# A one-core attention and mixture-of-experts kernel: the fourth chunk's sines and rotation after the third chunk's copies, and the output rows scaled one loop step later

## The chip, the cores and the metric

The kernel runs on one core of one Trainium2 chip. The metric is the device time of one launch in microseconds (us), the median over runs. A profile is one further execution, seen by the hardware profiler; its span runs from the first instruction to the last. Engines are called as in the profile: PE (matmuls), PEld (weight loads of PE), DVE (vector), ACT (scalar), POOL, and SP, which issues most DMAs. Each works through its own queue in order.

## What is computed

The input is x of 16 sequences with 512 rows of 128 numbers, all in float32. One layer is computed:

```
q, k = silu(x Wq), silu(x Wk), 16 heads of 8, rotated: [t*cos(ang), t*sin(ang)]
v    = x Wv
out  = (tril(q k^T) v) Wo * sigmoid(x G1 G2)      # linear attention, causal
x1   = layernorm(x + layernorm(out)*gamma + beta)
shared = (silu(x1 sg) * (x1 su)) sd               # for every row
routed = sum over the 2 best of 8 experts, 1280 rows per expert at most
y    = layernorm(x1 + shared + routed)
```

## The kernel before, in words

The 8192 rows are 64 chunks of 128 rows, four chunks to a sequence (`NC` = 4, `B` = 16, `NT` = 64). The order of the instructions on PE, ACT, DVE and POOL is the order in which the program writes them (`manual_schedule`), so every change of place in the code is a change of place in a queue.

**The attention loop** (L847 to L887) runs t from 1 to 64. In pass t it projects chunk t+2 (`project`: matmuls `products`; on ACT `squash`, `gate` and `spread`; on DVE `turn`, which writes the rotated `hat`), transposes chunk t+1 and copies it out of PSUM on ACT (`turn_over`: kT, q, qT), forms the causal products of chunk t (`energies`: 32 matmuls `pe` L526, four masked copies `et` L534 on DVE), and from them the output of chunk t-1 (`values`) and the running state (`remember`). Four of the eight PSUM buffers (`ps_w`) are handed round among all these tiles, so the projection of the next chunk waits until the copy `qT` (L488) has emptied an earlier buffer. The cosines and sines of the four chunk positions are made once, by `sines(c)` (one Abs and four Sin on ACT, L323 to L331), and `same(c)` on DVE duplicates them. For c = 3 this happens in pass t = 1, inside `project(3)`, and so ahead of the copies of chunk 2 on ACT; `turn(3)` follows it on DVE, ahead of the masked copies of chunk 1.

**The shared expert** is a list `feed` of small steps, 24 for each sequence: eight gate steps (`gate_half`: two matmul records L137 on PE and a Silu `sl` L139 on ACT), eight up steps (`up_half`: L150 on PE and the product `h` L151 on DVE), and eight down steps (`down_half`: L160; every second one ends with the addition L165 on DVE, which frees one of two PSUM buffers). They are written as 4 up-phase steps, then the 8 down steps of the sequence before, then 12 more up-phase steps.

**The expert phase** begins with six such steps, interleaved with expert 0's preparation in three parts of 512, 512 and 256 rows: `clear_rows` (L949, DVE) puts zero into unused rows, `turn_rows` transposes on PE (L960) and copies on DVE (L961). Then come eight experts, in which PE has no pauses.

**The tail** (L1106 to L1130) is the subject of two of the edits. Here 102 steps of `feed` are left. Each turn of the loop writes one of them, counts it in `begun`, and then writes some finishing work, if it has become due:

- `add_up(b)`: two additions L1017 on DVE that add the two routed rows of each token of sequence b; the second one also issues the load of a later sequence's rows.
- `finish_lot`: the last layernorm of four chunks. Four pairs of statistics (L105 and L107, DVE), the variance plus epsilon (`ve` L111, DVE), the power of minus one half on POOL (`rstd` L113), at least three steps later the product `nb` (L1041, DVE), then four scaled rows `res` (L1044, ACT) and a DMA of them (L1049, SP).

`an_end` advances the first of three running lots that isn't waiting; it is called up to twice in a turn, as often as `due` allows. `due` grows in each turn by the lots that are left times 9, divided by the steps that are left less 2. In the notation of the prediction a step is g, u or d with its sequence and number (u13.0 is the first up step of sequence 13; d12.2.0 is the first half of the third chunk's down product of sequence 12).

## Time and profile before

| | us |
|---|---|
| median of 3 runs | 841.85 (841.46 to 845.71) |
| the profiled execution, whole | 843.22 |
| its span | 841.5 |
| what lies outside the span | 1.7 |
| PE busy, of the span | 812.7 |
| DVE busy | 519.6 |
| ACT busy | 440.7 |
| POOL busy | 370.5 |
| attention, with the first shared steps | 0 to about 517 |
| experts | about 520 to 738 |
| tail | about 738 to 841.5 |

The profile gives each instruction a line of the kernel, the tiles that it writes and reads, and the idle time of its engine before it, with what ended that. A table of stretches gives the busy time of each engine and the clock that was granted to PE (1.00 is full). A list of waits gives who waited for whom: microseconds in total, times, longest. The timeline gives the start, the duration, the engine, the line, the operation and its tiles; an entry such as `[2.32 <-ACT qT L488]` at the end of a row says that the engine had been idle for 2.32 us and which instruction ended that.

### The profile page before, as it was taken

To read this page: it belongs to the slowest core of one execution; us is meant where nothing else is said; L and a number is where in the kernel's file an instruction comes from. 1 tells how busy PE (TensorE), PEld (TensorE's weight loads), DVE (VectorE), ACT (ScalarE), POOL (GpSimd) and SP (SyncE) were. 2 spreads that over 40 slices of the span, in tenths; PEclk is the share of its full clock that TensorE was granted. 3 is DMA by queue.
4 is the path that set the end of the run, shared out by engine and by line. 5 is a ranking of instruction groups with operands and counts; after the bars stand their busy time and mean duration, and the time that the engine had idled before them with its cause. 6 is when DMAs were issued, how large, how long until landed. Compare 5 with 4: busy or idle time off the path is not lost.

```text
span 841.5 us, 25752 instructions
## 1 busy us (share of the span) xinstructions
PE 812.7 (97%) x10290; PEld 555.6 (66%) x10290; DVE 519.6 (62%) x1603; ACT 440.7 (52%) x1413; POOL 370.5 (44%) x516
## 2 busy tenths in 40 slices
PE   6989999999999999999999999999999999999887
PEld 4766677668668667666666664766776677766555
DVE  7787777889977779965433335444344444247885
ACT  8677777786777778644222222333333333324545
POOL 2243333332377777878766570333333334312210
PEclk9999999999999999999999999999999999999999
DMA  6011111111111110075000015122321210034642
GB/s 205 23 35 35 35 34 34 35 34 34 32 44 60 50 52 30 26 269 204 25 11 7 2 29 144 32 83 92 98 76 43 92 63 30 26 109 138 177 124 63
DMA packets 66378, 57.54 MB, mean 68 GB/s; under 512 B 6164, under 2 KB 55116, under 8 KB 66258
## 3 DMA queue, kind: packets, MB, share of 16 engines
q1 hardware_dynamic: 59456, 44.95, 17.4%
q0 software_dynamic: 6656, 10.69, 3.7%
q8 instruction: 81, 1.33, 0.6%
q14 instruction: 39, 0.32, 0.1%
q10 hardware_dynamic: 146, 0.26, 0.1%
HBM read 32.62 MB, written 26.48 MB: 70 GB/s over the span
## 4 chain that ended last, share of the span: by engine, by line
PE 78%; DVE 13%; ACT 6%; issue 2%; POOL 0%; DVEq 0%; ACTq 0%; POOLq 0%
PE pd L160 11%; PE pu L150 10%; PE pg L137 10%; PE ped L984 8%; PE peg L1079 8%; PE peu L1081 8%; PE pq L426 5%; PE pe L526 3%; PE pt L479 3%; PE pout L559 2%; DVE h L151 2%; DVE et L534 2%; DVE st L105 2%; PE pst L500 2%; PE po L574 2%
## 5 line engine op out<-in xcount | busy, mean ns | idle before, releaser
L746 POOL DMA_INDIRECT xg_dram<-x,idx x128 | 130.2, 1017 | 41.0 <-issue 37.0
L990 POOL DMA_INDIRECT y_dram<-y,to x80 | 77.4, 967 | 160.9 <-ACT y L988 160.9
L151 DVE TENSOR_TENSOR h<-sl,pu 128x512 f32<-128x512 f32 x128 | 87.7, 686 | 89.3 <-PE pu L150 56.3
L139 ACT ACTIVATE sl<-pg 128x512 f32<-128x512 f32 x128 | 75.3, 595 | 122.0 <-PE pg L137 109.7
L160 PE MATMUL pd<-sd_sb,h 128*128 128x128 f32 x1024 | 125.4, 278 | 7.7 <-DVE x1T L165 7.5
L137 PE MATMUL pg<-x1T,sg_sb 128*128 128x512 f32 x256 | 131.7, 596 | 0.9 <-DVE h L151 0.8
L150 PE MATMUL pu<-x1T,su_sb 128*128 128x512 f32 x256 | 131.0, 593 | 0.0
L160 PEld LDWEIGHTS pd<-sd_sb,h 128*128 128x128 f32 x1024 | 120.8, 194 | 14.5 <-DVE x1T L165 8.4
L1084 DVE TENSOR_TENSOR eh<-esl,peu 128x512 f32<-128x512 f32 (+1 forms) x96 | 57.5, 599 | 109.7 <-PE peu L1081 98.7
L113 POOL TENSOR_TENSOR rstd<-ve,neghalf 128x4 f32<-128x4 f32 x47 | 49.2, 1046 | 142.8 <-DVE ve L111 107.0
L984 PEld LDWEIGHTS ped<-rd,eh 128*128 128x128 f32 x640 | 84.0, 192 | 24.1 <-issue 22.0
L534 DVE TENSOR_TENSOR et<-pe,causal 128x256 f32<-128x256 f32 x256 | 90.4, 416 | 4.8 <-PE pe L526 4.7
L511 POOL TENSOR_TENSOR state<-state,add 128x128 f32<-128x128 f32 x96 | 51.6, 538 | 76.5 <-DVE add L509 68.9
L1079 PE MATMUL peg<-xgT,rg 128*128 128x512 f32 (+1 forms) x192 | 84.6, 522 | 0.0
L1081 PE MATMUL peu<-xgT,ru 128*128 128x512 f32 (+1 forms) x192 | 84.4, 521 | 0.0
L984 PE MATMUL ped<-rd,eh 128*128 128x128 f32 x640 | 84.3, 275 | 0.0
L1083 ACT ACTIVATE esl<-peg 128x512 f32<-128x512 f32 (+1 forms) x96 | 50.6, 527 | 55.6 <-PE peg L1079 52.9
L150 PEld LDWEIGHTS pu<-x1T,su_sb 128*128 128x128 f32 x256 | 45.7, 190 | 44.4 <-issue 39.1
L988 ACT ACTIVATE y<-ped,wt 128x128 f32<-128x128 f32 x80 | 29.5, 369 | 85.6 <-PE ped L984 85.6
L137 PEld LDWEIGHTS pg<-x1T,sg_sb 128*128 128x128 f32 x256 | 44.1, 191 | 36.5 <-issue 32.3
L426 PE MATMUL pq<-W,xT 128*128 128x384 f32 x128 | 61.2, 561 | 5.8 <-ACT qT L488 4.6
L466 DVE TENSOR_TENSOR hat<-qk,cst_tok 128x512 f32<-128x512 f32 x64 | 46.4, 726 | 25.5 <-ACT qk L438 25.1
(184 smaller groups left out, 1266.3 us busy)
## 6 DMA issues: line engine op xcount, KB each, us to landing
y_dram<-vpad SPq DMA_DIRECT2D x16, 512.0 KB
y<-y_dram SPq DMA_DIRECT2D x32, 256.0 KB
xT<-xt SPq DMA_DIRECT2D x15, 384.0 KB
xg<-xg_dram SPq DMA_DIRECT2D x8, 660.0 KB
x<-x SPq DMA_DIRECT2D x16, 256.0 KB
o<-res SPq DMA_DIRECT2D x15, 256.0 KB
xg_dram<-x,idx POOLq DMA_INDIRECT x128
rg<-rg SPq DMA_DIRECT2D x8, 256.0 KB
```

The source lines that it names most:

```text
L137: nc.tensor.matmul(pg, sg_sb[:, ts(i, P)], seq, start=True, stop=True)
L139: nc.scalar.activation(sl, pg, AF.Silu)
L150: nc.tensor.matmul(pu, su_sb[:, ts(i, P)], seq, start=True, stop=True)
L151: nc.vector.tensor_tensor(h[i // half][:, i % half, :], h.pop(("s", i)), pu, ALU.mult)
L160: nc.tensor.matmul(pd, h[k][:, i - k * half, ts(c, P)], sd_sb[:, i, :], start=(i == 0), stop=(i == IS // P - 1))
L426: nc.tensor.matmul(pq[:, :, 0:24], xts[b][:, c, 0:P], W[:, 0:384].rearrange("p (h n) -> p h n", n=24), start=True, stop=True)
L534: nc.vector.tensor_tensor(et.rearrange("p s i n -> p (s i) n"), pes[a, half].rearrange("p s i n -> p (s i) n"), causal.unsqueeze(1).to_bro ...
L746: i = nc.gpsimd.indirect_dma_start(out=xg_dram[:, :], out_offset=bass.IndirectOffsetOnAxis(ap=idx[:, k, t : t + 1], axis=0), in_=x1[:, t, ...
L984: nc.tensor.matmul(pd, h[:, i, ts(c, P)], got[e][2][:, i, :], start=(i == 0), stop=(i == IR // P - 1))
L990: i = nc.gpsimd.indirect_dma_start(out=y_dram[:, :], out_offset=bass.IndirectOffsetOnAxis(ap=to[:, at : at + 1], axis=0), in_=y, in_offset ...
L1079: nc.tensor.matmul(pg[:, :n], rg_sb[:, ts(i, P)], xgTs[e][:, ds(o0, n)], start=True, stop=True)
L1081: nc.tensor.matmul(pu[:, :n], ru_sb[:, ts(i, P)], xgTs[e][:, ds(o0, n)], start=True, stop=True)
```

## The change

There are four edits. (1) `project(t)` no longer makes the sines and the rotation of chunks 0 to 3; those of chunk 3 are written in pass t = 1 after `energies(1)`, and so after the copies of chunk 2. In pass t = 2 `energies(2)` stands at the head of the pass, ahead of `project(4)`. (2) In `finish_lot`, after `nb`, at least one further step of `feed` is written before the scaled rows. (3) At the beginning of the expert phase the clearing of expert 0's third part stands behind the transposes and the copy of its first part. (4) The divisor of `due` is the number of steps that are left less 8, where it was less 2.

```
@@ project @@
-            if t == NC - 1:
-                sines(t)
-            turn(t)
+            if t >= NC:
+                turn(t)
@@ attention loop @@
                 stopped("wait")
+                if t == 2:
+                    energies(t)
                 if coming:
...
                 advance(turns)
-                if here:
+                if here and t != 2:
                     energies(t)
+                if t == 1:
+
+                    sines(NC - 1)
+                    turn(NC - 1)
                 if stopped("exp"):
@@ finish_lot @@
             nc.vector.scalar_tensor_tensor(nb, mv[:, :, 0], -1.0, rs, ALU.mult, ALU.mult)
+
+            at = begun
+            while not roots and feed and begun < at + 1:
+                yield False
             res = fp.tile([P, n, D], F32, tag="res", name=f"res_{lot[0]}")
@@ expert phase @@
-            for n_before, cleared in ((4, parts[:2]), (2, parts[2:])):
-                for _ in range(n_before):
-                    feed.pop(0)[2]()
-                for o0, n in cleared:
-                    clear_rows(0, o0, n)
-            for o0, n in parts:
-                turn_rows(0, o0, n)
+            for _ in range(4):
+                feed.pop(0)[2]()
+            clear_rows(0, *parts[0])
+            clear_rows(0, *parts[1])
+            for _ in range(2):
+                feed.pop(0)[2]()
+            turn_rows(0, *parts[0])
+            clear_rows(0, *parts[2])
+            turn_rows(0, *parts[1])
+            turn_rows(0, *parts[2])
             targets_of(0)
@@ tail @@
-                due += len(ends) * steps_each / max(len(feed) - 2, 1)
+                due += len(ends) * steps_each / max(len(feed) - 8, 1)
```

## The prediction

> **What bounds the kernel.** I read the page first (busy times, the slices, the chain that ended last).

> ```profile
> PE 812.7 (97%) x10290; PEld 555.6 (66%) x10290; DVE 519.6 (62%) x1603; ACT 440.7 (52%) x1413; POOL 370.5 (44%) x516
> ...
> PE   6989999999999999999999999999999999999887
> ...
> PE 78%; DVE 13%; ACT 6%; issue 2%; POOL 0%; DVEq 0%; ACTq 0%; POOLq 0%
> ```

> PE has work in 97% of the span, and only the first slices and the last three fall below nine tenths. So an edit can gain what PE stands idle there, and little else. I then went through PE's idle times in the timeline: 2.32 us at 19.4 to 21.7, and in the tail 1.93, 2.80 and 2.56 us, all before a down product L160. The list of waits for 740 to 842 says who causes these.

> ```profile
> ACT res L1044 <- DVE nb L1041: 34.6, 16, 5.0
> ...
> DVE h L151 <- ACT sl L139: 9.1, 8, 1.6
> ...
> PE pd L160 <- DVE x1T L165: 7.5, 4, 2.8
> ```

> PE waits 7.5 us for DVE's L165, and DVE itself, though late, stands idle 9.1 us in eight waits for an `sl` of ACT. The timeline of 754 to 772 shows such a wait and what becomes of it.

> ```profile
> 758.01 0.16 DVE L1041 SCALAR_TENSOR_TENSOR nb<-mv,rstd 128x4 f32<-128x4 f32 x1
> ...
> 758.20 0.88 ACT L1044 ACTIVATE res<-x1T,nb,rstd 128x128 f32<-128x128 f32 x2 [2.29 <-DVE nb L1041]
> ...
> 758.99 0.58 ACT L139 ACTIVATE sl<-pg 128x512 f32<-128x512 f32 x1
> ...
> 759.60 0.69 DVE L151 TENSOR_TENSOR h<-sl,pu 128x512 f32<-128x512 f32 x1 [1.43 <-ACT sl L139]
> ...
> 764.75 0.26 DVE L165 TENSOR_TENSOR x1T<-pd,x 128x128 f32<-128x128 f32 x1
> ...
> 765.07 5.47 PE L160 MATMUL pd<-sd_sb,h 128*128 128x128 f32 x32 [1.93 <-DVE x1T L165]
> ```

> ACT has `res` at its head, idle until `nb`; the `sl` behind it, whose matmul ended at 757.0, starts at 758.99; DVE idles 1.43 us; the lateness reaches L165 and PE. The other two stalls:

> ```profile
> 790.64 2.05 PE L160 MATMUL pd<-sd_sb,h 128*128 128x128 f32 x16 [2.80 <-DVE x1T L165]
> ```

> ```profile
> 814.77 4.11 PE L160 MATMUL pd<-sd_sb,h 128*128 128x128 f32 x32 [2.56 <-DVE x1T L165]
> ```

> The clock also counts. In the table of stretches it is halved after the stall at 763 and not after that at 788:

> ```profile
> 765.00:767.00 2.00, 1.93 (x11) 1.94 (x11) 1.72 (x7) 1.21 (x4) 1.01 (x1) 0.62 0.61 183
> 767.00:769.00 2.00, 2.00 (x11) 2.00 (x11) 0.48 (x2) 2.00 (x6) 0.00 (x0) 0.52 0.60 166
> ...
> 791.00:793.00 2.00, 1.84 (x17) 1.65 (x16) 1.86 (x10) 0.00 (x0) 0.23 (x1) 1.00 0.69 187
> ```

> **Edit 1, the start.** These are its rows:

> ```profile
> 18.87 0.36 ACT L323 ACTIVATE scratch<-scratch 128x192 f32<-128x192 f32 x1
> ...
> 20.28 0.37 ACT L481 COPY kT<-pt 128x256 f32<-128x256 f32 x1
> ...
> 21.08 1.41 DVE L534 TENSOR_TENSOR et<-pe,causal 128x256 f32<-128x256 f32 x4
> 21.27 0.38 ACT L488 COPY qT<-pt 128x256 f32<-128x256 f32 x1
> ...
> 21.71 1.65 PE L426 MATMUL pq<-W,xT 128*128 128x384 f32 x2 [2.32 <-ACT qT L488]
> ```

> The five sines hold ACT from 18.87 to 20.25, ahead of copies whose transposes had ended at 17.6. With the copies first, kT starts at 18.88, q at 19.14 and qT ends at 20.24 (21.65 now). DVE's `et` of chunk 1 start at 19.0, not 21.08, and end at 20.4. `energies(2)`, now at PE's head, needs q (20.0) and those `et`, and ends near 21.0; `project(4)`, behind it, starts there instead of 21.71. It takes 2.1 us now, at half clock after the idle time, and 1.14 at 26.43 at full clock. PE's idle time shrinks to 0.6, so I take 1.14: ACT's Silu of chunk 4 starts at 22.1, not 23.82. But sines and rotation come later: sines 20.25 to 21.63, `hat` of chunk 3 to 22.45 (now 21.16), its transposes near 23.1, and behind ACT's `spread` its kT at 23.5, where it is 25.05 now. The gain is **1.5 us**; at half clock it would be 0.6, and it can't exceed 2.9 (the idle time less 0.3, and 0.9 of slow projection). From there to 738 PE and the loop PE-ACT-qT set the pace, POOL's scatters hang on them, and the loads were issued long before, so the shift stays. SP's loads keep their order, since `energies` issues none.

> **Edit 3.** PE's third transposes now wait for the copy of part 1 (ends 519.88, they start at 519.93). Then they wait for the clearing of part 3, behind that copy: 518.84 + 0.60 + 0.43 = 519.87. **0.0**.

> **Edit 4** moves nothing. With 18 lots and 88 steps left `due` grows by 18*9/86 = 1.9 a turn and more later, and a turn uses two at most; counted through, only the 13th turn has one call where it now has two, and at that time every lot waits for its additions. The order written is the same. So the ends don't come sooner.

> **Edit 2** is what matters. I counted the loop through, before and after (for before this gives the order in which DVE's rows stand). `nb` keeps its place or moves a step, up to two statistics that followed `res` now stand directly behind it, and the `sl` of a gate step comes ahead of `res`. No instruction is added. DVE's starts lie apart by 0.60 (h, addition), 0.41 (statistics pair), 0.08 (nb), 0.1 (ve), 0.2 (L165); an `h` can start 1.13 after its up product does, an `sl` 1.06 after its gate product, and `res` takes 0.40 each.

> *First stall.* nb 758.01 stays. sl of g13.0 goes at 757.0, ahead of `res`. DVE does two statistics (to 758.9), h (759.5), addition (760.1), ve. ACT does `res` four times from 758.2 and the next sl to 760.35, so the last h starts at 760.4 instead of 761.82; the same 2.93 of work to L165 gives 763.3 for 764.75. The stall is 0.5, **1.4 less**. The next four half steps took 5.30 (765.07 to 770.37); four at full clock (0.89) take 3.57. After idle times of 0.85 and 0.89 (511, 519) the rows show 1.00, so I take the clock to stay full: **1.7**, bounds 0 and 1.7. DVE waits for PE there in either order, so the lateness starts anew at 0.

> *Second.* From the last L165 of sequence 12 to the first of 13 DVE has 17 statistics pairs, 8 additions and 8 h, before and after. Now it takes 19.55, of which 2.01 is waiting for `sl`. After, laid out in the same way, 0.55 is lost before the first h (two statistics that filled that time moved behind it) and 0.1 later. L165 comes 1.35 sooner; with half of the small waits among the following half steps (4.10 for 3.57) I count **1.9**.

> *Third.* DVE's wait is 2.61 of 18.86 now. After, one pair more, one wait of 0.55 (an `sl` behind two `res`), and a start 0.4 less late: L165 at 812.2 on the present scale, a stall of 0.2 to 0.3. With the small waits that follow (0.37, and 0.17 before 830.91) **2.8**.

> The tail's sum is 1.4 + 1.7 + 1.9 + 2.8 = 7.8; the most is 9.7 (7.5 of stalls, 1.7 of clock, 0.5), the least, if only the first stall shrinks, 1.4. What hides `res` coming later: at the end the last full lot's four rows end at 833.0 and ACT's next need is at 834.09. Each output DMA goes one or two steps later on SP, and a load may queue behind it, but a pair loaded at 752.4 is used at 764.9, 12 us later. If that cover were gone, DVE would wait at an addition.

> Sum: 1.5 + 0.0 + 0.0 + 7.8 = **9.3**. The profiled execution took 843.22 (span 841.5 and 1.7), which gives 833.9; the median is 1.4 lower and gives 832.6. I take **833.0**.

> **Rivals.** *(a) The clock falls elsewhere.* A stall of about 1.4 remains at 788, and the halved rows follow 1.93 but not 2.80, so length doesn't decide. If the halved stretch moves there and the start stays slow, the gain is 9.3 - 1.7 - 0.9 = 6.7: 835.4. [...]

> *(b) DVE is too late for the new place.* If `nb` runs over one half step (0.86) late, ACT stands at `res` as before, and the sl behind it waits. If stalls two and three stay, 1.5 + 1.4 + 1.7 = 4.6, without the clock 2.9: 837 to 839. For it: DVE is up to 4.6 late (pu ended at 808.5, h at 813.15). Against it: in my layout only one such wait is left.

> *(c) Slower.* The same lateness, but with four `res` in a row ahead of an `sl`, as at 827.33, where DVE idled 1.61. It decides when 8 of 14 lots pay it (12.9 against 9.1 now); with 12, 19.3 - 9.1 - 1.5 = 8.7 more: 850.5. My layout has four in a row for the lots at 758 and 808, ended in time.

> That edit 4 doesn't do what it says is in the forecast.

> **Chances.** Forecast 0.54 (its own range 829.5 to 836), (a) 0.17, (b) 0.21, (c) 0.08. Half a per cent is 4.2 us, about what a measurement of this kernel can tell from no change. Faster by more: forecast, (a) and a little of (b), 0.75; within: the rest of (b), 0.17; slower: 0.08. The low end 829.5 has the largest gains, 2.9 + 9.7 = 12.6 off 841.85, rounded up; the high end 838.5 takes in most of (b).

> **What would show it.** In the profile after: PE's idle time before L426 near 20 falls from 2.3 to 0.6 and the clock there stays at 1.00; DVE's wait for `sl` falls from 9.1 to below 3 and PE's wait for L165 from 7.5 to about 2; 765 to 770 has no halved clock; 517 to 738 is unchanged. I am wrong if DVE still waits for `sl` behind `res`, if additions wait for loads, or if the shift at the start is gone by 60 us.

## The result, and the profile after

| | before | after |
|---|---|---|
| median, us | 843.69 (841.46 to 845.71, 4 runs) | 833.06 (832.61 to 833.59, 4 runs) |
| ratio of the times | | 0.9876, 95% interval [0.9853, 0.9900] |
| the profiled execution, whole | 843.22 | 833.16 |
| its span | 841.5 | 831.4 |

The changed kernel is faster by 1.2%. To see where the time came from, I took matmuls that both kernels have and compared their starts in the two profiles. The projection of chunk 5 starts 2.20 us sooner, the work at 403 us 1.68 sooner, and the first expert's products behind edit 3 (at 520 us in the profile of before) 1.61 sooner. Nothing is gained or lost up to the tail (1.62). The tail gives the rest. The table cuts it at the third gate step of each sequence (g13.2 starts at 770.37 in before and at 765.66 in after), so each of the first three stretches holds one of the three stalls:

| us | g12.2 to g13.2 | g13.2 to g14.2 | g14.2 to g15.2 | g15.2 to the end | sum |
|---|---|---|---|---|---|
| before | 24.70 | 24.37 | 23.97 | 22.80 | 95.84 |
| after | 21.61 | 22.33 | 21.08 | 22.36 | 87.38 |
| gained | 3.09 | 2.04 | 2.89 | 0.44 | 8.46 |

1.62 and 8.46 make the 10.1 by which the spans differ. From the page of after, PE's row and the chain of work that ended last:

```profile
PE 810.5 (97%) x10290; PEld 554.8 (67%) x10290; DVE 519.3 (62%) x1603; ACT 439.6 (53%) x1413; POOL 369.0 (44%) x516
...
PE 82%; DVE 10%; ACT 5%; issue 1%; DMA 0%; DVEq 0%; ACTq 0%
```

PE has the same number of instructions and 2.2 us less of busy time (two halved-clock stretches are gone and one is new, below), and its share of the chain has grown from 78% to 82%: the kernel is nearer to what PE needs. The list of waits of after for the tail (us in total, times, longest):

```profile
ACT res L1053 <- DVE nb L1046: 17.9, 11, 4.2
...
DVE h L151 <- ACT sl L139: 1.9, 3, 1.0
...
PE pd L160 <- DVE x1T L165: 1.6, 2, 1.2
```

The first row was 34.6, the second 9.1 in eight waits, the third 7.5 in four. ACT still waits 17.9 us for `nb`, and that costs nothing any more, because DVE hardly waits behind it. The timeline of after shows the place where the first stall was:

```profile
756.39 0.15 DVE L1046 SCALAR_TENSOR_TENSOR nb<-mv,rstd 128x4 f32<-128x4 f32 x1
...
756.58 1.65 ACT L1053 ACTIVATE res<-x1T,nb,rstd 128x128 f32<-128x128 f32 x4 [0.57 <-DVE nb L1046]
...
758.13 0.57 ACT L139 ACTIVATE sl<-pg 128x512 f32<-128x512 f32 x1
...
758.74 0.69 DVE L151 TENSOR_TENSOR h<-sl,pu 128x512 f32<-128x512 f32 x1
...
761.67 0.26 DVE L165 TENSOR_TENSOR x1T<-pd,x 128x128 f32<-128x128 f32 x1
...
761.99 0.71 PE L160 MATMUL pd<-sd_sb,h 128*128 128x128 f32 x4 [0.46 <-DVE x1T L165]
```

`nb` is where it was (758.01 less the 1.62). ACT waits 0.57 for it, not 2.29, since the `sl` that stood behind `res` was done before. DVE's `h` has no idle time ahead of it, and PE's stall is 0.46 where it was 1.93. The stretches of after (us; busy time of PE, PEld, DVE, ACT, POOL; granted clock; DMA share; GB/s):

```profile
46.00:48.00 2.00, 2.00 (x44) 1.34 (x46) 1.97 (x6) 1.96 (x11) 0.00 (x0) 0.50 0.03 4
...
763.00:765.00 2.00, 2.00 (x21) 2.00 (x20) 1.40 (x5) 1.35 (x4) 0.69 (x1) 1.00 0.14 38
765.00:767.00 2.00, 2.00 (x12) 1.28 (x11) 1.52 (x7) 1.86 (x5) 0.00 (x0) 1.00 1.11 333
```

Behind the shorter stall the clock is full (it was 0.62 and 0.52). At 46 us it is halved once, where before had none. The projection at 47.00 us of before comes 2.26 sooner in after, the work at 61 us 1.33 sooner, so this stretch cost 0.9 us. At the start, the timeline of after:

```profile
18.80 0.37 ACT L480 COPY kT<-pt 128x256 f32<-128x256 f32 x1
...
19.97 1.06 PE L525 MATMUL pe<-q,kT 32*64 32x128 f32 x32 [0.68 <-ACT q L485]
...
20.95 0.91 PE L425 MATMUL pq<-W,xT 128*128 128x384 f32 x2
...
23.34 0.37 ACT L480 COPY kT<-pt 128x256 f32<-128x256 f32 x1
...
24.23 0.91 PE L425 MATMUL pq<-W,xT 128*128 128x384 f32 x2
```

The copy of chunk 2 starts at 18.80 and no longer at 20.28; the energies stand ahead of the projection, with 0.68 idle for 2.32, and the projection runs at full clock (0.91 for 1.65).

### The profile page after: what moved, and what is told of

The parts are those of the page before. It is cut to its first block, busy times and chain, and to the rows that moved or that the text cites. A ratio compares the mean times of both kernels' runs of the same rounds, so it can differ in the third digit from the quotient of the medians.

```text
span 831.4 us, 25754 instructions
## 1 busy us (share of the span) xinstructions
PE 810.5 (97%) x10290; PEld 554.8 (67%) x10290; DVE 519.3 (62%) x1603; ACT 439.6 (53%) x1413; POOL 369.0 (44%) x516
## 3 DMA queue, kind: packets, MB, share of 16 engines
q8 instruction: 81, 1.33, 0.7%
## 4 chain that ended last, share of the span: by engine, by line
PE 82%; DVE 10%; ACT 5%; issue 1%; DMA 0%; DVEq 0%; ACTq 0%
PE pd L160 13%; PE pu L150 11%; PE pg L137 11%; PE ped L989 9%; PE peg L1091 8%; PE peu L1093 8%; PE pq L425 5%; PE pe L525 3%; PE pt L478 3%; PE pout L558 3%; DVE et L533 2%; PE pst L499 2%; DVE h L151 2%; PE po L573 2%; DVE st L105 1%
## 5 line engine op out<-in xcount | busy, mean ns | idle before, releaser
L139 ACT ACTIVATE sl<-pg 128x512 f32<-128x512 f32 x128 | 76.0, 594 | 129.1 <-PE pg L137 114.4
L151 DVE TENSOR_TENSOR h<-sl,pu 128x512 f32<-128x512 f32 x128 | 87.5, 684 | 83.6 <-PE pu L150 57.4
L160 PE MATMUL pd<-sd_sb,h 128*128 128x128 f32 x1024 | 122.9, 276 | 1.7 <-DVE x1T L165 1.6
L160 PEld LDWEIGHTS pd<-sd_sb,h 128*128 128x128 f32 x1024 | 118.9, 192 | 7.8 <-issue 5.3
```

The lines of the kernel that those rows point to most:

```text
L139: nc.scalar.activation(sl, pg, AF.Silu)
L151: nc.vector.tensor_tensor(h[i // half][:, i % half, :], h.pop(("s", i)), pu, ALU.mult)
L160: nc.tensor.matmul(pd, h[k][:, i - k * half, ts(c, P)], sd_sb[:, i, :], start=(i == 0), stop=(i == IS // P - 1))
```

## The experiments

The theory under test: **the tail's gain comes from one place in one queue**. `res` stood at ACT's head before its `nb` was done, the Silu behind it came late, DVE waited for it and PE for DVE. The rivals: the gain comes from DVE's new order (the statistics that now stand behind `nb`); any delay of the lot's end gives it, however it is made; or the clock gives most of it. Smaller questions are whether edits 1, 3 and 4 do what the prediction says, and what still holds the tail back.

The kernels ran in three sets of four, each set on a chip of its own with the kernel before beside it, whose medians were 840.74 (23 runs), 843.50 (17 runs) and 840.68 (11 runs). Each ratio is against the kernel before of its own set.

### Edit 1 alone (set 1)

The diff is that of edit 1 in the change; the rest is before.

> Edit 1 alone on the kernel before. My theory (each edit pays for itself): the start gains 2.2 us at 26 us, as in the profile after, and 1.3 to 2.2 us of it reach the tail, depending on whether the clock is halved once more near 47 us; the tail keeps its three stalls of 1.9, 2.8 and 2.6 us and its 9.1 us of waiting for sl; in all 1.3 to 2.2 us less than before. Rival (the halved clock at 765 to 769 belongs to the phase of the kernel's clock window and not to the length of the stall): with the shift of the start alone the halved stretch at 765 vanishes, and the gain is 3.0 to 3.9 us.

Measured: 839.32, ratio 0.9979 [0.9967, 0.9991], 1.4 us below before. In its profile the work at 61 us is 2.43 sooner, and the tail shows the old stalls: 1.92, 2.79 and 2.30, with 8.9 us of waits `h <- sl`. But one thing was added there. From the stretches of this kernel:

```profile
787.00:789.00 2.00, 2.00 (x9) 2.00 (x10) 1.86 (x9) 0.00 (x0) 0.00 (x0) 0.50 0.78 217
```

The clock is still halved behind the stall of 1.92, so the rival, by which that halved stretch goes when the start shifts, did not come. (The clock window that the expectation names is seen in the profile of before as a grid: the halved stretches start at 11.15, 21.39 and 765.50 us, whole periods of 3.41 us apart.) It is now also halved behind the stall of 2.79, which went free in before (2.80 there), and that stretch of the tail took 25.37 for 24.37. The tail's code and the stall are the same; only the time at which they come has moved. Edit 1 alone thus gives what was forecast, and it can be taken back in part by where the clock falls.

### Edit 2 alone (set 1)

The diff is that of edit 2; the rest is before.

> Edit 2 alone on the kernel before. My theory: 7.8 to 8.5 us less; the stalls in the tail become 0.5, 1.2 and 0, DVE waits under 2.5 us for sl, and the clock at 765 to 769 is full because the stall before it is short. Rival (the phase of the clock window): the stall of 0.5 is followed by a halved clock as before, and the gain is 6.1 to 6.8 us.

Measured: 832.93, ratio 0.9904 [0.9887, 0.9920], 7.8 us below before. Its four stretches of the tail are 21.61, 22.33, 21.08 and 22.36, those of after to the hundredth. Edit 2 is the tail's whole gain, and edits 1 and 2 simply add up: 1.4 and 7.8 (after itself was 9.0 below before in set 3).

The rival that the clock gives most of it falls too. In two runs of this kernel and four of before in set 1 the mean granted clock was 0.999 or more; they took 832.46 and 832.61 against 839.07 to 839.44, so 6.5 to 7.0 us are left where the clock is full in both. The profiles say the same: the kernel with the sines alone (below) has the old order and a full clock through the whole tail, and takes 94.10 us there, 6.7 more than this one. The order gives about 6.7 us, and the rest is halved clock behind the old stalls.

### ACT's order alone (set 1)

Here DVE's order is exactly that of before; only the scaled rows and their DMA are held back until one further step has been written.

```
-                nc.scalar.activation(res[:, c, :], ...)
+                put(lambda c=c: nc.scalar.activation(res[:, c, :], ...))
...
-            nc.sync.dma_start(outv[:, lot[0] : lot[1], :], res)
+            put(lambda: nc.sync.dma_start(outv[:, lot[0] : lot[1], :], res))
...
+        def put(f):
+            held.append((begun + 1, f))
+            flush()
+        def flush():
+            while held and (roots or not feed or held[0][0] <= begun):
+                held.pop(0)[1]()
```

> On the kernel before: the scaled rows and their DMA are held back until the next shared step is written, while the lot itself goes on, so DVE's order is that of before and only ACT's order (and the output DMAs) changes. My theory (the gain comes from sl no longer standing behind res on ACT): 6.5 to 9 us less than before. Rival (it comes from the statistics that edit 2 moves behind DVE's L165, so that DVE has less to do before it): no gain, 0 to 1 us.

Measured: 833.89, ratio 0.9915 [0.9897, 0.9932]. The waits of this kernel's tail:

```profile
ACT res L1045 <- DVE nb L1041: 22.7, 16, 4.0
...
PE pd L160 <- DVE x1T L165: 1.2, 3, 0.6
DVE h L151 <- ACT sl L139: 1.2, 2, 0.8
```

DVE's waits for `sl` are gone with DVE's order untouched, and the tail takes 87.34 us (after: 87.38). The 1.0 us between the times of this kernel and the one above does not lie in the tail: their profiles show 0.45 of it, built up by 403 us in code that is the same in both, and I don't explain it. So the rival "DVE's new order" falls. One term of the prediction shows in passing: the second stall is 0.59 here and 1.18 in after, where two statistics that filled a wait have moved behind it (0.55 was forecast for that).

### The factor late too (set 1)

Everything is as in edit 2, except that `nb` itself is moved with its rows, so that `res` stands directly behind it as before.

```
-            while not roots and feed and begun < at + 3:
+            while not roots and feed and begun < at + 4:
                 yield False
             nb = small.tile([P, n], F32, tag="nb", name="nb")
```

> On the kernel before: nb waits four steps instead of three and res follows it at once. ACT's order and the places of the statistics are those of edit 2; only nb stands a step later on DVE. My theory (res must find its nb done, or ACT stands at res with sl behind it): part of the gain is lost, 2 to 6 us less than before, and DVE waits 4 to 8 us for sl. Rival (the place of the statistics and of res in the queues is all that counts): as edit 2 alone, 7.8 to 8.5 us less.

Measured: 843.67, ratio 1.0035 [1.0024, 1.0047]: 2.9 us above before, where 2 to 6 below was expected, and 10.7 above edit 2. The waits of its tail, and a place in its timeline:

```profile
ACT res L1044 <- DVE nb L1041: 28.5, 15, 5.3
...
DVE h L151 <- ACT sl L139: 9.8, 9, 1.5
PE pd L160 <- DVE x1T L165: 7.5, 3, 4.0
```

```profile
774.87 0.15 DVE L1041 SCALAR_TENSOR_TENSOR nb<-mv,rstd 128x4 f32<-128x4 f32 x1
...
775.07 1.65 ACT L1044 ACTIVATE res<-x1T,nb,rstd 128x128 f32<-128x128 f32 x4 [2.44 <-DVE nb L1041]
...
776.62 0.57 ACT L139 ACTIVATE sl<-pg 128x512 f32<-128x512 f32 x1
...
777.22 0.69 DVE L151 TENSOR_TENSOR h<-sl,pu 128x512 f32<-128x512 f32 x1 [1.18 <-ACT sl L139]
```

It is the old chain at a new place: ACT waits 2.44 us with `res` at its head, then does four rows, and only then the `sl`. The delay as such gives nothing; what gives the gain is **the distance between `nb` on DVE and `res` on ACT**. The rival "any delay" falls. The size was missed. The lateness now gathered in one stall of 3.97 us, and the clock was halved behind it and once more behind the third stall, of 2.27. These two stretches of the tail took 26.75 and 25.05; in the old order they take 24.34 and 23.93 at full clock (the sines alone). How much of the difference each halved stretch makes is not separated here. The first of them:

```profile
789.00:791.00 2.00, 2.00 (x11) 2.00 (x11) 1.19 (x5) 1.65 (x4) 0.00 (x0) 0.50 0.97 288
```

### Edit 4 alone (set 2)

The diff is that of edit 4. It leaves the order of the instructions as it was on PE, DVE, ACT, POOL and SP, so this run is a second sample of the kernel before.

> Edit 4 alone on the kernel before. My theory: the order written is that of before on every engine, so this is a second sample of the same program, 0.0 us, and shows how far two samples of one program lie apart. Rival (the ends do come sooner): a gain of over 1 us.

Measured: 844.84, ratio 1.0020 [1.0007, 1.0033]. The interval excludes 1, though nothing differs in any queue. Two samples of one program can lie 0.2% apart, and the interval of a ratio does not cover that. The times go with the clock that each run was granted: of the twelve here, the one at a mean of 0.998 took 842.34 us, and the four at 0.988 to 0.990 took 846.81 to 847.64. The profiles of the two differ in one thing that can be seen in the tail: the clock is halved behind the stall of 1.93 in before, and behind that of 2.80 here. A difference of 1.7 us or less needs the profile beside it.

### After once more (set 2), and two steps instead of one (set 2)

The first is after, unchanged, in a single run. The second is after with

```
-            while not roots and feed and begun < at + 1:
+            while not roots and feed and begun < at + 2:
                 yield False
             res = fp.tile([P, n, D], F32, tag="res", name=f"res_{lot[0]}")
```

> The changed kernel once more, for its profile. My theory (the halved clock depends on the phase of a window and not on the order of the work): the stalls of 0.5 and 1.2 us in the tail come again with a full clock, and the halved stretch at 45 to 49 us, which the kernel with edit 1 alone did not have, need not come again; the span is 830 to 832 us. Rival (the order of the work after edit 1 and 2 causes it): it comes again at the same place.

> On the changed kernel: two further steps between nb and the scaled rows instead of one. My theory (one step is nearly enough, and what is left of the stalls is DVE's own work): as the changed kernel within 1 us, that is 7.5 to 10.5 us less than before; DVE's wait for sl 0 to 2 us, the second stall near 1 us. Rival (the later the better): the second stall goes too, and it is 1 to 2 us below the changed kernel.

Measured: after again 832.96 in its one run, span 831.2, with a tail of 21.62, 22.33, 21.08 and 22.37; the clock at 46 to 48 us was full this time, and the work at 61 us was 2.84 sooner than in before (1.33 in the first profile of after). Two steps: 833.13, ratio 0.9875 [0.9861, 0.9889], no difference from after that can be measured. DVE's waits for `sl` fall further (0.7), the stalls of 0.46 and 1.18 go, and the second stretch takes 21.15; but a stall of 0.66 appears in the third (21.87 for 21.08). The expectation had left the second stall near 1 us; it went, as the rival said, but the 1 to 2 us that the rival put on it did not come: the tail is 0.8 us shorter (86.55), and the time shows none of it. One step is nearly enough for this loop, and what the second one gives is largely taken back where DVE is late for other reasons.

### Four additions on POOL (set 2)

This is after with the first addition of sequences 4, 6, 8 and 10 on POOL, which relieves DVE.

```
-                        nc.vector.tensor_tensor(rows, rows, pairs[b][:, k, c0:c1], ALU.add)
+                        eng = nc.gpsimd if k == 0 and b in (4, 6, 8, 10) else nc.vector
+                        eng.tensor_tensor(rows, rows, pairs[b][:, k, c0:c1], ALU.add)
```

> On the changed kernel: the first addition of the routed rows of sequences 4, 6, 8 and 10 is made by POOL, which is idle there, instead of DVE. My theory (the second stall of 1.2 us is DVE's work, 0.6 us for each addition): DVE reaches its L165 about 1.2 us sooner, the second stall falls below 0.4 us, and the time is 0.5 to 1.5 us below the changed kernel. Rival (POOL takes far longer than the 1.27 us of its addition of the same size in the attention, or slows DVE while it runs): the second addition waits for it, and the time is 0 to 3 us above the changed kernel.

Measured: 833.85, ratio 0.9888 [0.9873, 0.9902]. The second stall shrinks from 1.18 to 0.46 and the tail by 0.46 us (86.92), which is below what the times can tell. That is less than was expected (the stall below 0.4 us, the time 0.5 to 1.5 us below after); the single run of after in this set took 832.96. The group of POOL's additions (count, busy us, mean ns of one, idle time ahead):

```profile
L1023 POOL TENSOR_TENSOR x1T<-x1T,y 128x512 f32<-128x512 f32 x4 | 5.1, 1272 | 0.0
```

### The two halves of edit 1 (set 3)

The first kernel moves only the sines and the rotation of chunk 3, the second only `energies(2)` to the head of its pass; both are otherwise before.

```
             spread(t)
-            if t == NC - 1:
-                sines(t)
-            turn(t)
+            if t >= NC:
+                turn(t)
...
                     energies(t)
+                if t == 1:
+                    sines(NC - 1)
+                    turn(NC - 1)
```

```
                 stopped("wait")
+                if t == 2:
+                    energies(t)
...
-                if here:
+                if here and t != 2:
                     energies(t)
```

> On the kernel before, the first half of edit 1: the sines and the rotation of chunk 3 behind energies(1), energies(2) at its old place. My theory (the copies that stood behind the sines are what PE waited for): project(4) starts near 20.3 us instead of 21.7, and the copy kT of chunk 3 starts near 23.4 instead of 25.05; most of the start's gain, 1.3 to 2.2 us at 26 us. Rival (energies sooner gives the gain, by filling PE's idle time): under 0.5 us at 26 us.

> On the kernel before, the second half of edit 1: energies(2) ahead of project(4), the sines at their old place. My theory: energies(2) can't start before q of chunk 2 is copied at 21.4 us and project(4) starts behind it near 22.1, so kT of chunk 3 comes 0.2 to 0.6 us later than in the kernel before. Rival: a gain of 0.5 us or more at 26 us, since energies no longer stand behind the transposes.

Measured, one run each: 839.67 and 842.48, spans 838.0 and 840.8. The projections of chunks 4 and 5 in the timeline of the first:

```profile
20.28 0.91 PE L425 MATMUL pq<-W,xT 128*128 128x384 f32 x2 [0.95 <-ACT qT L487]
...
24.91 0.91 PE L425 MATMUL pq<-W,xT 128*128 128x384 f32 x2
```

The energies of chunk 2 in the timeline of the second:

```profile
22.22 1.56 PE L526 MATMUL pe<-q,kT 32*64 32x128 f32 x32 [1.90 <-ACT qT L488]
```

With the sines alone, the projection of chunk 5 starts 1.52 sooner than in before (24.91 for 26.43). With the energies alone it starts at 27.91, 1.5 later (0.2 to 0.6 was expected): the copies still stand behind the sines, so the energies wait at PE's head (1.90 here) and hold the projection back. With both it starts at 24.23. The clock has a part in these starts: it was halved from 21.39 to 24.80 in before and from 24.32 to 27.73 with the energies alone, and full there with the sines alone and with both. So not all of the 1.52 is order, but the last comparison is at full clock on both sides: moving the energies is a loss without the sines and worth another 0.7 with them.

### A better version (set 3)

This is after with two steps, with the four additions on POOL and with edit 3 undone, beside after itself.

```
-            turn_rows(0, *parts[0])
             clear_rows(0, *parts[2])
+            turn_rows(0, *parts[0])
             turn_rows(0, *parts[1])
```

> The changed kernel with two steps between nb and the rows, the four additions on POOL, and edit 3 undone. My theory (by the profiles of the two single trials the tail gets 0.8 and 0.4 us shorter, and edit 3 costs 0.1): no stall over 0.5 us in the tail and 0.8 to 1.5 us less than the changed kernel timed beside it. Rival (what is left of DVE's lateness is not what ends last): within 0.5 us of it.

> The changed kernel, timed on the same chip as the version above, for a direct comparison: 9 to 11 us less than before.

Measured: 830.23 (829.4 to 830.7, 5 runs), ratio 0.9877 [0.9857, 0.9897], and after 831.72 (830.58 to 832.28, 6 runs), ratio 0.9893 [0.9874, 0.9911]. The better version is 1.5 us below after. That is less than the 0.2% of the twin above, so the times alone would not carry it. Its profile does: the tail takes 21.15, 20.88, 21.52 and 22.37, 85.92 in sum, against 87.35 for after on the same chip, 1.4 less. In the list of its waits, PE's for L165 is down to one:

```profile
PE pd L160 <- DVE x1T L165: 0.3, 1, 0.3
```

The two measures, which gave 0.8 (two steps) and 0.5 us (POOL) of the tail alone, give 1.4 together.

## Why the prediction was right

**Edit 1, forecast 1.5.** Alone it gave 1.4, and in the profile of after it stands at 1.61 behind edit 3. The steps came where the prediction put them: the projection of chunk 4 at 20.95 (forecast 21.0), the copy kT of chunk 3 at 23.34 (23.5), idle time 0.68 (0.6), full clock. Where the shift is first seen whole, at the projection of chunk 5, it is 2.20, and it didn't all last: in the profile of after the halved clock at 46 us took 0.9. That 1.61 was left, so near to 1.5, is in part luck. The condition that would have made the prediction wrong, a shift gone by 60 us, did not come: seven profiles with edit 1 whole show 1.33 to 2.84 there; edit 2 alone, ACT's order alone and edit 4 alone show between -0.06 and 0, the sines alone 0.56 and the energies alone -1.37.

One run without edit 1 stands out: with the factor late the work at 61 us is 1.01 sooner than in before, because its clock stayed full at the start, where that of before was halved from 21.39 to 24.80. It lets the two terms of edit 1 be told apart. The runs with two steps and of after in set 3 have the same full clock from 17.3 us on, and their copy qT at 17.3 comes 0.1 sooner than in that run; they start the projection of chunk 5 at 24.73 and 24.74, that run at 25.52. So the new order alone is worth about 0.7, where the prediction had 0.6 (its gain at half clock). The clock is worth 1.4, where it had 0.9: from the projection of chunk 4 to that of chunk 5 before takes 4.72 us and the run with the factor late 3.28. The prediction counted only the slow projection, but the halved stretch also held the transposes behind it (1.06 for 0.60).

**Edit 3, forecast 0.0.** PE idles 0.97 to 0.98 us ahead of the third transposes in five profiles with the edit (after, after again, two steps, POOL, after in set 3) and 0.88 to 0.89 in the nine without. It costs 0.09: the clearing now ends last, where the copy did. The prediction had both end within 0.01 us of each other, so this was a term that it could not resolve; it stays far below what can be timed.

**Edit 4, forecast nothing.** Right: the order written is the same. The 1.0020 measured for it is a size of the spread between samples, not of the edit.

**Edit 2, forecast 7.8, measured 8.46 in the profile and 7.8 by its own run.** By its terms: first stall and clock 3.1 forecast, 3.09 measured (stall 0.46 for the 0.5 forecast, clock full behind it). Second 1.9, measured 2.04. Third 2.8 with the small waits behind it, of which 0.17 in the last stretch; measured 2.89 and 0.44. The last stretch is the largest miss, 0.27. It is one place: in before the matmul at 830.91 waits for `h`, which was late behind four `res`. Matmuls of this product start 0.11 us apart and last 0.28, so a start that comes 0.45 after the one ahead of it is 0.33 late, though the profile shows only 0.17 of idle time before it, and the next start lost 0.10 more. The prediction took the idle time for the loss. The two runs with moved `nb` and with ACT's order alone show that the mechanism is the one named and not merely a matching sum. Only the 1.7 of clock belongs to this one profile of before: its first stretch took 24.70, and 23.05 to 23.07 with edit 4, the sines or the energies alone, where the clock was full. By the tails of the five profiles with the old order, 94.10 to 96.55, edit 2 is worth 6.7 to 9.2.

**Rival (a), the clock falls elsewhere.** It happened in part and not where the rival put it. Behind the stall of 1.18 that remains at the second place the clock stayed full in every profile, but in the profile of after it was halved at 46 us, and in two other profiles of after it was not. The length of the stall alone did not decide it: the halved stretch stands behind the stall of 1.93 in before and behind that of 2.80 with edit 4 alone, in the same order of instructions, and each lies on the grid of its own trace (last section). A stall of 1.92 us was enough (edit 1 alone), in a period of 3.41 us in which PE was busy for 0.44 of the time. The 835.4 that the prediction put on this rival is a slip: a gain of 6.7 gives 835.6 from the start that its 833.0 implies.

**Rival (b), DVE too late for the new place.** DVE's waits for `sl` came out at 1.9 us (below 3 was forecast), so it did not happen. The run with the factor moved shows that it was a real danger: there DVE's waits are 9.8 us.

**Rival (c), four `res` in a row ahead of an `sl`.** It did not decide anywhere: four in a row stand at 756.58 in after, and were done in time.

That the forecast of 833.0 met the measured 833.06 so closely is luck. Counted from the profiled execution, the 9.3 us gave 833.9, and the profiles differ by 10.1; counted from the median of before it gave 832.6, and that median was 841.85 then and 843.69 with a fourth run.

## What to carry to other kernels

When two engines feed each other in fixed order, look for an instruction that waits at the head of one queue for the other engine, and ask what stands behind it: the cost is not its own wait but that of the work it holds up (in after ACT still waits 17.9 us for `nb`, but DVE's waits for `sl` fell from 9.1 to 1.9). Moving it back paid here only where what it waits for stayed in its place: edit 2 alone took 832.93 us, with `nb` moved along it took 843.67. Two moves can depend on each other, as the sines and the energies do (the projection of chunk 5 came 1.52 sooner with the sines alone and 1.5 later with the energies alone), so a half tried alone may be slower than nothing. And a stall on PE can cost more than its length: behind the one of 1.93 us the halved clock cost another 1.6 here, and whether it did was not decided by the stall's length alone, so compare kernels at the same granted clock.

## What the runs showed of the hardware

```profile
762.09:765.50 3.41, 1.48 (x13) 1.29 (x12) 3.24 (x12) 0.00 (x0) 0.90 (x1) 1.00 0.36 100
765.50:768.91 3.41, 3.41 (x18) 3.41 (x17) 1.61 (x8) 3.12 (x8) 1.01 (x1) 0.50 0.52 150
785.98:789.39 3.41, 1.86 (x17) 1.67 (x15) 3.27 (x13) 0.70 (x3) 0.49 (x1) 1.00 0.29 87
789.39:792.80 3.41, 2.05 (x16) 1.86 (x16) 3.24 (x14) 1.09 (x3) 0.54 (x2) 1.00 0.84 241
```

  With edit 4 alone it is the other way round: an edge at 765.79 cuts the first stall (busy 0.50 in the period before it), and nearly all of the second lies in one period (0.26), behind which the clock is halved from 789.68.
- **A drift common to a whole set.** Between 224 and 403 us, in code that no edit touches, each kernel gains or loses against the first profile of before by about the same amount as the others of its set, which ran on the same chip: 0.7 to 1.1 us gained in set 1, 0.9 to 1.1 lost in set 2, 1.1 gained in set 3. The cause is open; comparisons there hold only within a set.
- **An addition of 128x512 took 1.27 us on POOL and 0.68 on DVE.** DVE's own additions of that size kept their mean (677 ns in after, 680 in the kernel with four on POOL), but none of them ran at the same time as one of POOL's in the tail. Two short instructions of DVE that did were held up: `nb` at 764.87 took 0.68 us and `ve` at 789.97 took 0.63, where their medians are 0.16 and 0.17, and both ended 0.02 to 0.03 after POOL's addition did. In the better version `ve` took 0.52 and 0.31 and ended in the same way. The statistics beside POOL kept their times (0.26 to 0.29).
